# Queries and keys turned on VectorE and through DRAM, two groups ahead, from the 57th group on

## The chip, the cores and the metric

The kernel runs on one core of one Trainium2 chip. The metric is device time of one execution in microseconds. Everything is fp32. Engine names are those of the profile: PE is TensorE's matmul (PEld its weight loads), DVE VectorE, ACT ScalarE, POOL GpSimd; SP is the SyncE queue, from which all DMAs here are issued.

## The reference

Input x is [2, 4096, 256]. First comes a recurrent mixing layer (queries, keys and values from x and x shifted by one token, a running log-sum-exp over the 4096 tokens, a group norm, an output projection), added to x. Its result is normalised and goes through two layers of windowed attention with a gated MLP, and the sum is the output. Per layer (8 heads of 64, windows of 128 tokens, each window seeing itself and the one before):

```python
h = shift_token(x)
q, k, v = jnp.split(h @ wqkv, 3, axis=-1)        # 256 -> 3 x 512
q = l2norm(q) * qs;  k = l2norm(k) * ksc
q, k = rotary_xpos(q, k)
o = local_attention(q, k, v)                     # softmax over up to 129 keys
x = x + o @ wo
h = layernorm(shift_token(x)) ;  a, g = split(h @ w1 + b1)
x = x + (a * gelu(g)) @ w2 + b2
```

## The kernel before

**Work.** After the recurrence of the first batch (some 240 us, the kernel's start), the attention layers go over 128 groups of 128 tokens (NN = 128; group n is window n % 4 of block n // 4, four groups to a block of 512 tokens). The blocks run batch by batch, and in a batch layer by layer: 8 blocks of layer 0, then 8 of layer 1. The recurrence of the second batch is woven into groups 5 to 54.

**One group**, in the loop at L1540, written as iteration n: group n's scores, softmax and turning of probabilities; group n + 1's projection; group n - 1's fetch of turned probabilities; group n - 2's values, output projection and residual; and a part of the MLP of an earlier block (fill, L1412).

- project (L1033): 128 tokens times wqkv, 512 columns each for q, k and v, out of PSUM into qk (two buffers) or vt.
- square, rotate, norms, cosines, rotated (L1062 to L1104): norm and rotary position. ACT squares qk into the tile sq (one buffer); POOL multiplies the rotated halves into t2; DVE reduces sq to rn, POOL takes rn to the power -1/2; DVE writes the cosine products over sq, adds t2 to it, and writes sq times rn back into qk.
- transpose_qk (L1106): PE transposes qk in eight 128x128 blocks (four for k, four for q) into two PSUM banks, and ACT or DVE copies them into kT and qT. kT has three parts: 1 and 2 for even and odd groups; after an odd group part 2 is copied to part 0 by a DMA, so that a group always finds the window before it just ahead of its own.
- scores (L1130): 32 matmuls (64 records of fp32, as two passes) of 32 queries by 160 keys, eight at a time in parts of the array, and behind them, in one piece, values of group n - 2 (L1250).
- softmax (L1156), turn_p (L1203): the probabilities are transposed in 32x32 blocks on DVE (tile turned), written to DRAM (pd), and fetched in the turned order (fetch_p, L1226, four DMAs into pT; plan.turned, L250, is the view that does it). values reads pT and pB as its moving operand.
- shift, normed, transpose_h (L1287 to L1328): the shifted residual for the MLP, by four DMAs a group.

**Order.** No engine's order is written out by hand. Every call is noted as an operation of a plan (L274) with a cost (L338); order() (L412) runs all engines in a list schedule by those costs, picks at each step the operation of the lowest iteration among those that can start, gives out the eight PSUM banks and decides for "either" copies between ACT and DVE. The instructions are then written in that order, and each engine works through its own strictly in turn. A changed cost or a changed operation can so move instructions anywhere. A DMA's cost is this line, with 170 bytes a nanosecond:

```python
o.passes = size / 170 if ways == 16 else size / (25 * ways)
```

Nearly all instructions bear the line of the helper that writes them (L566), so groups are known by their tiles.

Of the kernel before, what the change touches and what calls it, by code (L numbers as in the profile page):

```python
# [33 lines left out]
MASKED = -3e38  # L34
R_SLOTS = 50
AHEAD = 10
SPLIT = 3
INSIDE = 2

# [154 lines left out]
class Plan:  # L194
# [143 lines left out]
    def cost(self, o):  # L338

        views = [*o.outs, *o.ins]  # L340
        n = max([v.idx.size for v in views] or [1])
        psum = any(v.place.psum for v in views)
        inside = sum(v.idx.size == n and not v.place.psum for v in o.ins)
        o.set, o.lock, o.half, o.passes, name, hold = None, False, "full", 0, o.name, None
        if o.eng == "tensor":
            trans = name == "transpose"
            left = o.args[1]
            move = o.args[2] if len(o.args) > 2 else o.args[1]
            cols = max(move.idx.size, left.idx.size) if not trans else P
            o.step = (1 if trans else 2) * (cols / 1.2 + (2 if cols >= 256 else 3))  # L350
            rows, cols = (P // max(n, 32) if n <= 64 else 1 for n in (left.shape[0], left.idx.size))
            if not trans and rows * cols > 1:
                o.half = "part" if rows > 1 and cols > 1 else "row" if rows > 1 else "col"
                o.step /= rows * cols
            o.time = o.step + 150
        elif o.eng == "vector":
            d = 150 + 1.04 * n
            if name == "tensor_tensor_reduce":
                d = 240 + 1.04 * n
            elif name == "tensor_tensor_scan":  # L360
                d, o.lock = 203 + 2.1 * n, True
            elif name == "scalar_tensor_tensor":
                d, o.lock = 200 + 1.05 * n, inside > 1
            elif name == "tensor_tensor":
                o.lock = inside > 1
            elif name == "tensor_scalar":
                d, o.lock = 155 + (1.27 if psum else 0.98) * n, not psum and n > 16
            elif name == "tensor_copy" and not psum:
                d, o.lock = 230 + 0.45 * n, n > 16
            elif name == "bn_aggr":  # L370
                d = 172
            elif name == "transpose":
                d = 170 + 1.04 * n
            elif name == "reciprocal":
                d = 147 + 4 * n
            o.step, o.time = max(d - 85, 60), d
        elif o.eng in ("scalar", "either"):
            d = (160 if psum else 195) + 0.83 * n
            if name == "scaled":
                d = 305 + 0.76 * n  # L380
            elif name == "activation":
                o.set = SETS.get(o.args[2])
                if o.args[2] == AF.Identity:
                    d = 365 + 0.87 * n
                elif isinstance(o.kw.get("bias"), View):
                    d += 85
            o.step, o.time = d - 100, d
            if "accum_out" in o.kw:
                o.time = d + 200
        elif o.eng == "gpsimd":  # L390
            o.lock = name != "memset"
            if name == "tensor_tensor":
                d = 430 + 156 * n if ALU.pow in o.args else 140 + 2.22 * n
            elif name == "tensor_scalar":
                d = 230 + 1.12 * n
            else:
                d = (100 if name == "memset" else 187) + 0.98 * n
            o.step, o.time = d, d
            hold = d if n > 64 else 100
        else:  # L400
            v = min(views, key=lambda v: v.shape[0] * v.idx.size)
            size = 4 * v.shape[0] * v.idx.size
            rows = max(v.shape[0] if v.shape[0] > 1 else v.shape[1] for v in views)
            ways = max(k for k in range(1, 17) if rows % k == 0)
            o.passes = size / 170 if ways == 16 else size / (25 * ways)
            inner = len(views) == 2 and not any(v.place.outer for v in views)
            o.step = 370 if not inner else 580 if ways in (1, 16) else 800
            o.time = LAND + o.passes
        o.hold = hold or o.time
# [160 lines left out]
def kernel(ctx: ExitStack, tc: tile.TileContext, a: dict, out: bass.AP):  # L570
# [331 lines left out]
    w2 = tile_of([P, NM, D], "w2")  # L902

    def weights(l, which):
        if "qkv" in which:
            for j in range(3):
                cols = slice(j * INNER, (j + 1) * INNER)
                nc.sync.dma_start(out=wqkv[:, :, cols], in_=a["w_qkv"][l][:, :, cols])
        if "o" in which:
            nc.sync.dma_start(out=wo, in_=a["w_o"][l])  # L910
        if "1" in which:
            nc.sync.dma_start(out=w1, in_=a["w_1"][l])
        if "2" in which:
            nc.sync.dma_start(out=w2, in_=a["w_2"][l])


    kT = tile_of([P, HEADS // 2, 3, W], "kT")

# [6 lines left out]
    G_LAST = 5  # L927
    blocks = [(l, b, c) for b in range(B) for l in range(L) for c in range(NB)]
    xs, xTs, hs, x1s, zs, hTs, rems, pys = ({} for _ in range(8))
    tabs, qks_of, vts, qTs, pos, sims, prs, pTs, pBs, dvs, sqs, t2s = ({} for _ in range(12))  # L930


    def load(k):
# [161 lines left out]
    def rotated(n):  # L1095
        qk = qks_of[n]
        (u, rn), t2 = sqs.pop(n), t2s.pop(n)
        nc.vector.tensor_tensor(u, u, t2, ALU.add)
        nc.vector.tensor_tensor(
            qk.rearrange("p j h d -> p (j h) d"),  # L1100
            u.rearrange("p j h d -> p (j h) d"),
            rn.unsqueeze(2).to_broadcast([P, 2 * HEADS, DH]),
            ALU.mult,
        )  # L1104

    def transpose_qk(n):  # L1106
        qk = qks_of.pop(n)
        qT = qTs[n] = tile_of([P, HEADS // 2, P], "qT", 2)
        me = 1 + n % 2
        for j, dst in ((1, kT[:, :, me, :]), (0, qT)):  # L1110
            pt = bank([P, HEADS // 2, P])
            for hp in range(HEADS // 2):
                nc.tensor.transpose(
# [1 line left out]
                    qk[:, j, 2 * hp : 2 * hp + 2, :].rearrange("p h d -> p (h d)"),  # L1115
                    ident,
                )
            either(dst, pt)
        if me == 2:
            nc.sync.dma_start(out=kT[:, :, 0, :], in_=kT[:, :, 2, :])  # L1120

    def lone(n):

# [6 lines left out]
    def scores(n):  # L1130

        qT = qTs[n]
        me = 1 + n % 2
        seen = W if lone(n) else 2 * W
        ks = slice(me, me + 1) if lone(n) else slice(me - 1, me + 1)
        sims[n] = [bank([P, 2, 2 * W]) for _ in range(4)]
        with piece():
            down_ends(n - 1)  # L1140
            for hp in range(HEADS // 2):
                for q, r in product(range(NQ), range(2)):
                    s, m = divmod(hp, 2)
                    rows, toks = slice(r * DH, (r + 1) * DH), slice(q * SQ, (q + 1) * SQ)
                    keys = slice(0, W) if lone(n) else slice(q * SQ, q * SQ + W + SQ)
                    nc.tensor.matmul(
                        sims[n][2 * s + r][toks, m, 2 * W - seen : 2 * W][:, keys],
                        qT[rows, hp, toks],
                        kT[rows, hp, ks, :].rearrange("p c j -> p (c j)")[:, keys],
                        start=True,  # L1150
                        stop=True,
                    )
# [375 lines left out]
    mixed_out(0)  # L1528
    transpose_x(0)
    load(1)  # L1530
    table(0)
    for j in range(3):
        project(0, j)
    square(0)
    rotate(0, 0)
    rotate(0, 1)
    norms(0)
    cosines(0)
    rotated(0)
    for n in range(NN + 3):  # L1540
        k, w = divmod(n, NW)
        o = n - 1
        ko, wo_ = divmod(o, NW)
        here, ahead, behind = n < NN, n + 1 < NN, 1 < n <= NN + 1
        plan.at(n)
        if here:
            transpose_qk(n)
        for c in range(rec2.n):
            if NW + 1 + int(c * R_SLOTS / rec2.n) == n:
# [7 lines left out]
                    rec2.group_norm()  # L1557
        plan.at(n)

        first, l = ahead and (n + 1) % (NB * NW) == 0, ((n + 1) // (NB * NW)) % L  # L1560
        if w == 3 and k + 2 < NK:
            load(k + 2)
        if w == 0 and k + 1 < NK:
            mixed_out(k + 1)
        if n > 2:
            normed(hs[(n - 3) // NW][:, (n - 3) % NW, :])
        if ahead:
            table(n + 1)
            if first:
                weights(l, "qkv")  # L1570
            project(n + 1, 0)
            rotate(n + 1, 0)
        if here:
            scores(n)
        else:
            with piece():
                if n < NN + 2:
# [7 lines left out]
        if here:  # L1585
            softmax(n, 0)
            softmax(n, 1)
        if ahead:
            project(n + 1, 1)
            square(n + 1)  # L1590
            rotate(n + 1, 1)
        if behind:
            output(n - 2)
            shift(n - 2)
# [1 line left out]
                weights(o // (NB * NW) % L, "o")  # L1596
        if wo_ == 1 and 0 < ko < NK:
            transpose_h(ko - 1)
        if w == 2 and k + 1 < NK:
            transpose_x(k + 1)  # L1600
        if here:
            softmax(n, 2)
            softmax(n, 3)
        if ahead:
            norms(n + 1)
        fill(o, 0)
        if here:
            turn_p(n, 0)
        if ahead:
            project(n + 1, 2)  # L1610
            cosines(n + 1)
        fill(o, 1)
        if here:
            turn_p(n, 1)
        if ahead:
            rotated(n + 1)
        fill(o, 2)
        fill(o, 3)
        if wo_ < 2 and NW < o < NN and (o - NW - wo_) % (NB * NW) == 0:
# [83 lines left out]
```

## Time and profile before

| | us |
|---|---|
| median of 3 runs | 2783.24 (2782.43 to 2784.07) |
| profiled execution, its own time | 2785.52 |
| its span | 2783.8 |
| PE / DVE / ACT / POOL busy in it | 2741.1 / 2173.9 / 1894.2 / 1676.8 |
| scores of group 0 / 56 / 127 begin | 243.1 / 1364.5 / 2708.1 |

A group's length is the distance between the starts of two bursts of kT,qT matmuls on PE's timeline. It varies from 13 to 23 us with the share of the MLP that falls into it. The granted TensorE clock is 0.995 over the span. In rows of groups the columns are: line, engine, operation, out<-in, shapes, count, then busy us and mean ns of one, then the idle time of the engine just before them and what ended it. Matmuls are pipelined: the length of one record overlaps the next.

### The profile page before, as it was taken

To read this page: it belongs to the slowest core of one execution; us is meant where nothing else is said; L and a number is where in the kernel's file an instruction comes from. 1 tells how busy PE (TensorE), PEld (TensorE's weight loads), DVE (VectorE), ACT (ScalarE), POOL (GpSimd) and SP (SyncE) were. 2 spreads that over 40 slices of the span, in tenths; PEclk is the share of its full clock that TensorE was granted. 3 is DMA by queue.
4 is the path that set the end of the run, shared out by engine and by line. 5 is a ranking of instruction groups with operands and counts; after the bars stand their busy time and mean duration, and the time that the engine had idled before them with its cause. 6 is when DMAs were issued, how large, how long until landed. Compare 5 with 4: busy or idle time off the path is not lost.

```text
span 2783.8 us, 61393 instructions
## 1 busy us (share of the span) xinstructions
PE 2741.1 (98%) x21356; PEld 1752.8 (63%) x21356; DVE 2173.9 (78%) x4651; ACT 1894.2 (68%) x5079; POOL 1676.8 (60%) x1959
## 2 busy tenths in 40 slices
PE   9999999999999999999999999999999999999998
PEld 4476656656666666666666666666665666666666
DVE  7888989998988888888776776677776777776663
ACT  7887767777777776676666666666666666666663
POOL 2226666667666666766665665666666666666661
PEclk9999999999999999999999999999999999999999
DMA  2224535444443444333435443343334444334331
GB/s 82 104 69 166 174 108 156 124 121 135 138 127 101 144 115 121 106 99 114 121 117 153 131 151 115 110 122 110 114 104 125 138 130 118 113 117 123 108 100 47
DMA packets 414365, 332.13 MB, mean 119 GB/s; under 512 B 61412, under 2 KB 377572, under 8 KB 413544
## 3 DMA queue, kind: packets, MB, share of 16 engines
q1 hardware_dynamic: 414056, 328.20, 39.5%
q8 instruction: 170, 2.79, 0.4%
q14 instruction: 139, 1.14, 0.1%
HBM read 153.01 MB, written 108.99 MB: 94 GB/s over the span
## 4 chain that ended last, share of the span: by engine, by line
PE 80%; DVE 2%; ACT 2%; issue 0%; DMA 0%; POOL 0%; SPq 0%; DVEq 0%; ACTq 0%
PE bank L566 80%; ACT pr L566 1%; DVE arena L566 1%; DVE qk L566 0%; ACT pr L562 0%; ACT arena L566 0%; DVE sq L566 0%; ACT L566 0%; DVE turned L566 0%; DVE hm L566 0%; ACT hm L566 0%; DVE rn L566 0%; ACT oT L566 0%; DVE bank L566 0%; ACT ends L566 0%
## 5 line engine op out<-in xcount | busy, mean ns | idle before, releaser
L566 PE MATMUL bank<-wqkv,xT 128*128 128x512 f32 x1536 | 711.8, 597 | 4.5 <-POOL xT L566 4.0
L566 PE MATMUL bank<-hT,w 128*128 128x512 f32 (+2 forms) x1452 | 636.3, 582 | 0.0
L566 POOL TENSOR_TENSOR t<-qk,tab 128x256 f32<-128x256 f32 x512 | 393.4, 788 | 278.5 <-ACT qk L566 228.8
L566 PEld LDWEIGHTS bank<-wqkv,xT 128*128 128x128 f32 x1536 | 280.4, 191 | 284.9 <-issue 269.4
L566 ACT ACTIVATE pr<-bank,nmx 128x129 f32<-128x129 f32 (+1 forms) x1024 | 367.7, 379 | 130.3 <-DVE nmx L566 113.5
L566 PEld LDWEIGHTS bank<-hT,w 128*128 128x128 f32 (+1 forms) x1452 | 269.7, 189 | 274.0 <-issue 254.0
L566 POOL TENSOR_TENSOR rn<-rn,mhalf 128x16 f32<-128x16 f32 x128 | 390.8, 3053 | 5.7
L562 ACT ACTIVATE pr<-pr,sums 128x129 f32<-128x129 f32 (+1 forms) x972 | 325.3, 421 | 19.5 <-DVE sums L566 19.2
L566 POOL TENSOR_SCALAR_AFFINE_SELECT pB<-pT 127x512 f32<-127x512 f32 x248 | 238.3, 976 | 143.0 <-DMA pT<-pd 105.7
L566 DVE COPY_PREDICATED bank<-fronts,bank 128x254 f32<-128x254 int32 x496 | 187.8, 418 | 171.6 <-PE bank L566 171.2
L566 ACT COPY qk<-bank 128x512 f32<-128x512 f32 x222 | 130.5, 588 | 250.2 <-PE bank L566 232.6
L566 PE MATMUL bank<-w,hm 128*128 128x256 f32 x1280 | 298.5, 382 | 0.0
L566 PEld LDWEIGHTS bank<-w,hm 128*128 128x128 f32 x1280 | 237.8, 190 | 35.6 <-issue 6.0
L566 PE MATMUL bank<-wo,oT 128*128 128x256 f32 x1024 | 242.5, 380 | 1.4 <-ACT oT L566 1.3
L566 PEld LDWEIGHTS bank<-wo,oT 128*128 128x128 f32 x1024 | 194.1, 190 | 58.1 <-issue 19.6
L566 DVE STREAM_TRANSPOSE turned<-pr 128x512 f32<-128x512 f32 (+1 forms) x380 | 195.2, 538 | 40.4 <-ACT pr L562 38.7
L566 ACT ACTIVATION_READ_ACCUMULATOR pr<-bank,nmx 128x1 f32 x1024 | 221.5, 216 | 0.0
L566 ACT COPY hm<-bank 128x512 f32<-128x512 f32 (+1 forms) x175 | 100.8, 576 | 175.0 <-PE bank L566 174.9
L566 DVE TENSOR_REDUCE rn<-sq 128x16 f32<-128x1024 f32 x128 | 155.0, 1211 | 71.1 <-ACT sq L566 69.9
L566 PE MATMUL bank<-pT,vt 128*64 128x128 f32 x2048 | 203.4, 279 | 0.0
L566 POOL TENSOR_TENSOR dv<-dv,vt 127x512 f32<-127x512 f32 x124 | 177.0, 1428 | 30.4 <-DMA dv<-vt 23.4
L566 DVE TENSOR_REDUCE nmx<-bank 128x2 f32<-128x258 f32 x496 | 192.6, 413 | 0.1
(154 smaller groups left out, 5106.2 us busy)
## 6 DMA issues: line engine op xcount, KB each, us to landing
pd<-turned SPq DMA_DIRECT2D x256, 256.0 KB
pT<-pd SPq DMA_DIRECT2D x512, 128.0 KB
dv<-vt SPq DMA_DIRECT2D x124, 224.0 KB
tab<-in_c_rot_dram SPq DMA_DIRECT2D x128, 128.0 KB
kT<-kT SPq DMA_DIRECT2D x64, 256.0 KB
z<-zd SPq DMA_DIRECT2D x16, 512.0 KB
x<-in_x_dram SPq DMA_DIRECT2D x16, 512.0 KB
x1d<-x SPq DMA_DIRECT2D x16, 512.0 KB
```

Source lines behind the costliest of these rows:

```text
L562: self.nc.scalar.activation(dst, src, AF.Copy, scale=scale)
L566: getattr(getattr(self.nc, o.eng), name)(*args, **kw)
```

## The change

Up to group 55 all stays as it was, but for the layout of kT and qT: both are now cut into blocks of 32 tokens (block, head pair, token) where they were (head pair, part, token), and the copies out of PSUM write that layout.

From group 56 on (FAR = 56):

- Iteration n projects q and k of group n + 2 instead of n + 1 (v stays at n + 1), with all steps up to rotated. At iteration 54 the chain of group 56 is done once more, whole (rotated_now), to start this off.
- transpose_qk is gone. In its place turn_qk, right behind rotated: two transposes on DVE in 32x32 blocks, qk (q, then k) into the tile sq, whose content is no longer wanted, and one DMA of the 512 KB to a DRAM buffer qd (three of them).
- fetch_qk, right behind the scores of the iteration before its own: eight DMAs of 64 KB out of qd, four into kT and four into qT, each for one block of 32 rows, in runs of 512 bytes.
- A block's x is transposed one group sooner (w == 1 in place of 2). At a change of layer the weights of q and k are loaded apart from those of v, since they are wanted a group apart.

For all groups, the plan's cost of a DMA goes from 170 to 270 bytes a nanosecond. The sum of DVE transposes added is 144, of DMAs 72 writes and 576 fetches, of PE transposes removed 576.

```diff
+FAR = 56
-            o.passes = size / 170 if ways == 16 else size / (25 * ways)
+            o.passes = size / 270 if ways == 16 else size / (25 * ways)
...
-    kT = tile_of([P, HEADS // 2, 3, W], "kT")
+    kT = tile_of([P, 3 * NQ, HEADS // 2, SQ], "kT")
+    qds = [plan.dram([P, 2 * INNER], f"qd_{i}") for i in range(3)]
...
     def rotated(n):
+        turns[n] = u
...
+    def rotated_now(n):
+        table(n)
+        project(n, 0)
+        project(n, 1)
+        square(n)
+        rotate(n, 0)
+        rotate(n, 1)
+        norms(n)
+        cosines(n)
+        rotated(n)
...
+    def turn_qk(n):
+        qk, u = qks_of.pop(n), turns.pop(n).rearrange("p j h d -> p (j h d)")
+        for j in range(2):
+            to = u.rearrange("p (b j c) -> p b j c", b=NQ, j=2)[:, :, j, :]
+            of = qk[:, j].rearrange("p h d -> p (h d)")
+            nc.vector.transpose(
+                to.rearrange("p b (h t) -> p b h t", t=SQ),
+                of.rearrange("p (h b d) -> p b h d", b=NQ, d=SQ),
+            )
+        nc.sync.dma_start(out=qds[n % 3], in_=u)
+
+    def fetch_qk(n):
+        qT = qTs[n] = tile_of([P, NQ, HEADS // 2, SQ], "qT", 2)
+        for b in range(NQ):
+            bs = slice(b * SQ, (b + 1) * SQ)
+            for j, dst in ((1, kT[bs, mine(n)]), (0, qT[bs])):
+                nc.sync.dma_start(
+                    out=dst.rearrange("p a h t -> p a (h t)"),
+                    in_=plan.turned(qds[n % 3], (2 * b + j) * P, 0, P),
+                )
+        kept_keys(n)
...
+    def kept_keys(n):
+        if n % 2:
+            nc.sync.dma_start(out=kT[:, :NQ], in_=kT[:, 2 * NQ :])
...
                     nc.tensor.matmul(
-                        sims[n][2 * s + r][toks, m, 2 * W - seen : 2 * W][:, keys],
-                        qT[rows, hp, toks],
-                        kT[rows, hp, ks, :].rearrange("p c j -> p (c j)")[:, keys],
+                        sims[n][2 * s + r][toks, m, o : o + wide * SQ],
+                        qT[rows, q, hp, :],
+                        kT[rows, b0 : b0 + wide, hp, :],
...
+        m = n + 1 if n + 1 < FAR else n + 2
+        comes = m < NN
         plan.at(n)
-        if here:
+        if n < min(FAR, NN):
             transpose_qk(n)
...
-        if ahead:
-            table(n + 1)
-            if first:
-                weights(l, "qkv")
-            project(n + 1, 0)
-            rotate(n + 1, 0)
+        if comes:
+            table(m)
+            if m % (NB * NW) == 0:
+                weights(m // (NB * NW) % L, "qk")
+            project(m, 0)
+            rotate(m, 0)
         if here:
             scores(n)
+            if FAR <= n + 1 < NN:
+                fetch_qk(n + 1)
...
-        if w == 2 and k + 1 < NK:
+        if w == (1 if (k + 1) * NW >= FAR else 2) and k + 1 < NK:
             transpose_x(k + 1)
...
-        if ahead:
-            rotated(n + 1)
+        if comes:
+            rotated(m)
+            if m >= FAR:
+                turn_qk(m)
+        if n + 2 == FAR:
+            rotated_now(FAR)
+            turn_qk(FAR)
```

More of the change, by code (lines that the diff above doesn't have):

```diff
@@ L904, in weights @@
     def weights(l, which):
-        if "qkv" in which:
-            for j in range(3):
+        for j, t in enumerate("qkv"):
+            if t in which:
                 cols = slice(j * INNER, (j + 1) * INNER)
@@ L929 @@
     xs, xTs, hs, x1s, zs, hTs, rems, pys = ({} for _ in range(8))
-    tabs, qks_of, vts, qTs, pos, sims, prs, pTs, pBs, dvs, sqs, t2s = ({} for _ in range(12))
+    tabs, qks_of, vts, qTs, pos, sims, prs, pTs, pBs, dvs, sqs, t2s, turns = ({} for _ in range(13))
     def load(k):
@@ L1104, in rotated @@
         )
+    def rotated_now(n):
[8 more added lines that the diff above has]
+        rotated(n)
     def transpose_qk(n):
         qk = qks_of.pop(n)
-        qT = qTs[n] = tile_of([P, HEADS // 2, P], "qT", 2)
-        me = 1 + n % 2
-        for j, dst in ((1, kT[:, :, me, :]), (0, qT)):
+        qT = qTs[n] = tile_of([P, NQ, HEADS // 2, SQ], "qT", 2)
+        for j, dst in ((1, kT[:, mine(n)]), (0, qT)):
             pt = bank([P, HEADS // 2, P])
@@ L1117, in transpose_qk, with mine @@
                 )
-            either(dst, pt)
-        if me == 2:
-            nc.sync.dma_start(out=kT[:, :, 0, :], in_=kT[:, :, 2, :])
+            either(dst.rearrange("p a h t -> p h a t"), pt.rearrange("p h (a t) -> p h a t", t=SQ))
+        kept_keys(n)
[10 more added lines that the diff above has]
+    def fetch_qk(n):
+        qT = qTs[n] = tile_of([P, NQ, HEADS // 2, SQ], "qT", 2)
+        for b in range(NQ):
[5 more added lines that the diff above has]
+                )
+        kept_keys(n)
+    def mine(n):
+        me = 1 + n % 2
+        return slice(me * NQ, (me + 1) * NQ)
+    def kept_keys(n):
+        if n % 2:
+            nc.sync.dma_start(out=kT[:, :NQ], in_=kT[:, 2 * NQ :])
     def lone(n):
@@ L1130, in scores @@
     def scores(n):
[L1134 to L1137, printed above, removed]
+        qT = qTs.pop(n)
         sims[n] = [bank([P, 2, 2 * W]) for _ in range(4)]
@@ L1144, in scores @@
                     rows, toks = slice(r * DH, (r + 1) * DH), slice(q * SQ, (q + 1) * SQ)
-                    keys = slice(0, W) if lone(n) else slice(q * SQ, q * SQ + W + SQ)
+                    own = mine(n).start
+                    b0, wide = (own, NQ) if lone(n) else (own - NQ + q, NQ + 1)
+                    o = W if lone(n) else q * SQ
                     nc.tensor.matmul(
-                        sims[n][2 * s + r][toks, m, 2 * W - seen : 2 * W][:, keys],
-                        qT[rows, hp, toks],
-                        kT[rows, hp, ks, :].rearrange("p c j -> p (c j)")[:, keys],
+                        sims[n][2 * s + r][toks, m, o : o + wide * SQ],
+                        qT[rows, q, hp, :],
+                        kT[rows, b0 : b0 + wide, hp, :],
                         start=True,
@@ L1530 @@
     load(1)
[L1531 to L1539, printed above, removed]
+    rotated_now(0)
+    project(0, 2)
     for n in range(NN + 3):
@@ L1558 @@
         plan.at(n)
-        first, l = ahead and (n + 1) % (NB * NW) == 0, ((n + 1) // (NB * NW)) % L
         if w == 3 and k + 2 < NK:
@@ L1587 @@
             softmax(n, 1)
-        if ahead:
-            project(n + 1, 1)
-            square(n + 1)
-            rotate(n + 1, 1)
+        if comes:
+            project(m, 1)
+            square(m)
+            rotate(m, 1)
         if behind:
@@ L1603 @@
             softmax(n, 3)
-        if ahead:
-            norms(n + 1)
+        if comes:
+            norms(m)
         fill(o, 0)
@@ L1609 @@
         if ahead:
+            if (n + 1) % (NB * NW) == 0:
+                weights((n + 1) // (NB * NW) % L, "v")
             project(n + 1, 2)
-            cosines(n + 1)
+        if comes:
+            cosines(m)
         fill(o, 1)
@@ L1614 @@
             turn_p(n, 1)
-        if ahead:
-            rotated(n + 1)
+        if comes:
+            rotated(m)
[4 more added lines that the diff above has]
+            turn_qk(FAR)
         fill(o, 2)
```

## The prediction

> **What bounds the kernel now.** I read the views in this order: the page's engine table and chain of waits, the windows by stage, the groups by form, PE's timeline over two groups of the steady part, and the DMA issues of the SP queue. The page first:
>
> ```profile
> span 2783.8 us, 61393 instructions
> PE 2741.1 (98%) x21356; PEld 1752.8 (63%) x21356; DVE 2173.9 (78%) x4651; ACT 1894.2 (68%) x5079; POOL 1676.8 (60%) x1959
> PE 80%; DVE 2%; ACT 2%; issue 0%; DMA 0%; POOL 0%; SPq 0%; DVEq 0%; ACTq 0%
> ```
>
> PE is busy almost throughout and carries the chain that ended last; the next owners of that chain have 2% each. An average may hide stages, so the windows come next. Group 56, the first that the change treats otherwise, begins its scores at 1364.5 us (the 57th burst of kT,qT matmuls on PE's timeline), group 124 at 2657.5. Columns: length, busy us of each engine, granted clock, share of the DMA engines, GB/s.
>
> ```profile
> 400.00:1364.50 964.50, 954.17 (x7684) 611.08 (x7680) 847.55 (x1738) 709.54 (x1900) 628.68 (x715) 0.99 0.42 122
> 1364.50:2658.00 1293.50, 1293.50 (x10805) 826.94 (x10807) 928.87 (x2062) 828.69 (x2381) 829.13 (x927) 1.00 0.41 122
> 2658.00:2783.80 125.80, 117.22 (x900) 82.59 (x884) 59.45 (x137) 56.74 (x168) 41.60 (x48) 0.97 0.26 77
> ```
>
> In the middle row PE is busy 1293.50 of 1293.50 us: for 68 groups it never waits, whatever the others do. A group lasts 1293.5 / 68 = 19.02 us there; DVE works 928.87 / 68 = 13.66 us of it (72%), ACT and POOL 12.2 us each (64%). So in this stage time is PE's work, and only what leaves PE's list counts, as long as the other engines keep it fed.
>
> **What the change takes from PE.** Eight 128x128 transposes a group (transpose_qk) for groups 56 to 127: 72 x 8 = 576, and the instruction lists of the two programs differ on PE by just these. Their price must not be read from the mean of one (274 ns, the first row below), which counts a pipelined instruction from start to end, nor from busy time / count (131 ns), which has the last one's tail in it. It is the distance between starts on PE's timeline (start, length, what, count):
>
> ```profile
> L566 PE MATMUL bank<-mats,qk 128*128 128x128 f32 x1024 | 134.2, 274 | 9.7 <-DVE qk L566 9.7
> ...
> 1805.07 1.34 PE L566 MATMUL bank<-kT,qT 64*32 64x160 f32 x64
> 1806.34 0.44 PE L566 MATMUL bank<-pT,vt 128*64 128x128 f32 x4
> 1806.61 0.39 PE L566 MATMUL bank<-pB,dv 128*64 128x128 f32 x4
> 1806.83 0.39 PE L566 MATMUL bank<-pT,vt 128*64 128x128 f32 x4
> 1807.05 0.39 PE L566 MATMUL bank<-pB,dv 128*64 128x128 f32 x4
> ...
> 1825.54 1.04 PE L566 MATMUL bank<-mats,qk 128*128 128x128 f32 x8
> 1826.41 1.88 PE L566 MATMUL bank<-wqkv,xT 128*128 128x512 f32 x4
> ```
>
> From 1825.54 to 1826.41 the eight take 0.87 us of PE; the same 0.87 stands at nearly every group after 1000 us. 72 x 0.87 = **62.6 us** less PE work.
>
> The Trainium skill speaks against such a change: "VectorE: DVE Perf Modes", Rules for kernel authors, gives 128x128 transposes to TensorE where a PSUM destination will do, and The three transpose paths there puts one at 390 ns in bf16. By that figure 576 of them would be an estimated 225 us of PE; this trace's starts, 109 ns apart, decide for 62.6.
>
> **The scores with the new layout (all 128 groups).** Keys are now read as four or five pieces of 32 floats, 512 bytes apart, in place of one run. The nearest row is pT/pB: they are read as four pieces of 32, 1 KB apart, and four records of 128 columns, two side by side, start 0.22 us apart: 4 x 128 / 2 / 0.22 = 1160 columns per us, where 512 contiguous columns take 0.43 us (1190). So pieces cost nothing that shows. Value taken: 0. Bounds: 0, and half speed, 1.25 us a group (64 records, median distance of starts) x 128 = 160 us.
>
> **What goes to the others, from group 56 on.** Prices by these rows:
>
> ```profile
> L566 DVE STREAM_TRANSPOSE turned<-pr 128x512 f32<-128x512 f32 x256 | 180.8, 706 | 40.4 <-ACT pr L562 38.7
> L566 ACT COPY kT<-bank 128x512 f32<-128x512 f32 x115 | 67.5, 587 | 29.9 <-PE bank L566 29.2
> ...
> 1832.97 1.52 SPq L566 DMA_DIRECT2D pT<-pd  x3
> 1838.23 0.53 SPq L566 DMA_DIRECT2D pd<-turned  x1
> ```
>
> - DVE gains two block transposes of 128x512 (turn_qk): 2 x 0.706 = 1.41 us, so 13.66 + 1.41 = 15.07 us. The group shrinks to 19.02 - 0.87 = 18.15 us: 83%.
> - ACT loses nearly all of two copies out of PSUM, 2 x 0.59 = 1.18 us, and two PSUM banks are free earlier. ACT falls to 11.0 of 18.15 us (61%). No gain is counted: ACT is not the bound.
> - SP issues nine more DMAs: one write of 512 KB (as pd<-turned, 0.50 us each over this stage) and eight fetches (as pT<-pd, 0.48): 4.4 us. Added up over 1364 to 2700 us its issues hold 753 us of SP, 10.7 us a group; they become 15.1 of 18.15, again 83%.
> - The DMA engines: 1024 packets of 512 B (27.6 ns each, mean of such packet records here) and 128 of 4 KB (189 ns) are 52 us, over 16 engines 3.3 us a group. The share goes from 0.41 to (0.41 x 19.02 + 3.3) / 18.15 = 0.61.
> - POOL keeps its work.
>
> **New idle time of PE.** None of this is on PE, and the projection two groups ahead gives the turned keys a whole group to arrive. But all engines run in a written order and DVE is fuller. The trace has both ends: at 72% DVE PE idles 0; between 400 and 1364.5 us, with DVE at 847.55 / 964.5 = 88%, it idles 10.33 us in 48 groups, 0.21 a group. At 83% a straight line gives 0.15 a group, 72 x 0.15 = **10.7 us**. Bounds: 0, and 1 us in each of some 36 short groups, half of the 72 (rival 1). If the cover is gone, each microsecond of wait per group costs 72.
>
> **The other edits.** The planner's DMA rate (170 to 270) and the new copies reorder the whole program, the first 1364 us too; the 10.3 us of PE idle there may halve or double: -5 to +10, taken as 0, since a reordering has no sign that I can read. At iteration 54 a whole extra chain for group 56 (rotated_now) falls where DVE is at 88%: its DVE work, some 6.8 us (1.21 + 2 x 0.73 + 1.34 + 1.34 + 1.41), comes sooner, not on top; 0 to 5 us, taken as 0 because PE has a group's work ahead of it. The weights loaded in two parts: before, PE idles nothing at groups 64 and 96; 0. The fewer DMA pieces of the kept keys: off the path, 0. In the last 125.8 us PE idles 8.6; projecting earlier leaves PE less to fill with there, up to +3, in the range.
>
> **Sum.** The profiled execution took 2785.52 us, 1.7 more than its span; the median shown is 2783.24. All terms are differences of span, so they are put on the median: 2783.2 - 62.6 + 10.7 = **2731.3 us**.
>
> **Rivals.**
> 1. *SP becomes the late one.* For: 15.1 us of issues against short groups (from the scores of 56 to those of 57 it was 13.7 us, and one or two in four are 13 to 17), while pT, dv and the eight fetches all become ready together just behind the scores, 8.5 us in one queue. Against: the long groups, 20 to 23 us, let it catch up, and SP idles 45% now. If each of the 36 short groups loses 1 us: 2731 + 36 = 2767.
> 2. *The one sq buffer closes a loop (slower than before).* The turned block lies in sq, and the next group's square on ACT has to wait until the write to DRAM has read it. Behind square in ACT's order stand the exponentials, and behind those the scores' banks and PE. The loop: square 1.07, reduction 1.21, POOL's power 0.44 + 3.05, product 1.34, turning 1.41, issue 0.50, landing some 3.6 (pT<-pd 2.56 in the chain, plus 1.5 - 0.4 for the larger transfer, an estimate from the packet records): 12.6 us. It binds when waits in DVE's, ACT's and SP's queues add over 18.15 - 12.6 = 5.5 us a group, and from 6.4 us on the result is slower than before. With 7 us of waits a group takes 19.6: 2783 + 72 x 0.58 = 2825. Against: two of three queues have 17% free, the third 39%.
> 3. *Keys in pieces run slower*: half speed would be 2731 + 160 = 2891. The pT row speaks against it.
> 4. *The change doesn't do what it says*: PE finds other waits at once, and the time stays at 2783. Against: 68 groups without a gap.
>
> **The numbers.** My forecast case (2715 to 2748) has 0.72; below it, with the early idle gone too, 0.03; rival 1 and the upper part of its cost (2748 to 2777) 0.10; rival 4 (within 0.2%, about what a measurement can tell from no change: 2777.7 to 2788.8) 0.04; rival 2 has 0.09, rival 3 0.02. Faster 0.72 + 0.03 + 0.10 = 0.85, same 0.04, slower 0.11. The low end is 2783.2 - 62.6 - 5 = 2715; the upper end goes to rival 1's 2767, so that about 2 in 10 stay outside.
>
> **What would show it.** Right: 448 transposes (mats,qk) left on PE in place of 1024, PE still over 98% busy between group 56 and 124 with some 18.2 to 18.4 us a group, sq<-qk transposes near 0.7 us, kT,qT still 1.25 us a group, the DMA share near 0.6. Wrong: PE idle before kT,qT released by DMA kT<-qd (rival 1), ACT idle before sq released by DMA qd<-sq (rival 2), or kT,qT over 1.4 us a group (rival 3). The prediction fails most easily at the 0.15 us of idle a group, which is a line drawn through two points.

## The result, and the profile after

The changed kernel took 2813.99 us (median of 4, 2807.84 to 2818.15), the kernel before 2783.64 (4 runs, 2782.43 to 2784.07): ratio 1.0108, 95% interval 1.0087 to 1.0129. It is **slower by 30 us**; 2731.3 with a range up to 2767 was forecast. Below, each measured time is followed by its ratio and the 95% interval of it; differences in us are differences of such ratios, each to the kernel before on the same chip, times 2783. By the intervals such a difference is uncertain by some 6 us.

The page of the changed kernel:

```profile
span 2806.1 us, 60848 instructions
PE 2708.9 (97%) x20780; PEld 1703.0 (61%) x20780; DVE 2274.6 (81%) x4814; ACT 1818.0 (65%) x4916; POOL 1683.2 (60%) x1959
PE 6%; DVE 3%; SPq 3%; ACT 3%; DMA 2%; issue 1%; POOL 1%; POOLq 0%; DVEq 0%; ACTq 0%
```

PE has 576 instructions less, as forecast. But the chain that ended last, followed back over some 19% of the span here, is no longer PE's (80% of the span before): SP, DVE and ACT have half of PE's share each, and DMAs 2%. By stage (length, busy us of PE, PEld, DVE, ACT, POOL, granted clock, DMA share, GB/s):

```profile
397.00:1349.50 952.50, 947.14 (x7765) 609.21 (x7764) 845.95 (x1742) 703.68 (x1890) 625.79 (x711) 1.00 0.42 125
1349.48:2676.14 1326.66, 1268.36 (x10226) 780.83 (x10225) 1027.71 (x2205) 761.72 (x2237) 842.57 (x929) 0.99 0.58 172
```

The first row ends sooner than before (group 56 starts its scores at 1349.5 instead of 1364.5). The second, groups 56 to 123, was 1293.0 us (1364.5 to 2657.5) with PE busy throughout; now it is 1326.7 and PE idles 58.3 us. So the stage that should have shrunk by 59 grew by 34. The two largest waits of PE there (us in total, times, longest):

```profile
PE bank L567 <- ACT oT L567: 24.3, 14, 3.4
PE bank L567 <- DMA qT<-qd: 18.9, 16, 2.5
```

The second row is the fetch itself arriving late. The first is something else: output projections that wait for ACT's copy of oT. Why ACT is late is seen further up the stream. DVE's longest list of waits in this stage, after:

```profile
DVE st L567 <- DMA h<-x: 133.5, 48, 7.5
```

and in the same groups before:

```profile
DVE st L566 <- DMA h<-x: 63.5, 14, 5.8
```

h<-x is the shifted residual of the MLP, four pieces a group, a transfer that the change does not touch. One such case, on all engines' timeline of the changed kernel (start, length, engine, what, count, [idle before <- releaser]):

```profile
2071.22 1.20 SPq L567 DMA_DIRECT2D h<-x  x2
2072.51 1.08 SPq L567 DMA_DIRECT2D pd<-turned  x2
2073.68 0.40 SPq L567 DMA_DIRECT2D kT<-qd  x1
...
2076.99 0.43 SPq L567 DMA_DIRECT2D qT<-qd  x1
...
2077.47 1.46 SPq L567 DMA_DIRECT2D h<-x  x2
...
2080.32 0.43 DVE L567 BATCH_NORM_STATS2 st<-h 128x6 f32<-128x256 f32 x1 [3.03 <-DMA h<-x]
...
2082.10 1.31 DVE L567 STREAM_TRANSPOSE sq<-qk 128x512 f32<-128x512 f32 x2
...
2083.33 0.72 DVE L567 COPY_PREDICATED bank<-fronts,bank 128x254 f32<-128x254 int32 x2
...
2084.47 0.37 ACT L567 ACTIVATE pr<-bank,nmx 128x129 f32<-128x129 f32 x1 [5.58 <-DVE nmx L567]
...
2084.83 0.58 ACT L567 COPY oT<-bank 128x512 f32<-128x512 f32 x1
...
2085.46 1.35 PE L567 MATMUL bank<-wo,oT 128*128 128x256 f32 x5 [0.74 <-ACT oT L567]
```

Read it down. Two pieces of h are issued at 2071.2; then the eight fetches hold SP from 2073.68 to 2077.42, back to back, and the last two pieces of h come only behind them. DVE's statistics of h wait 3.03 us for those. DVE works in turn, so what stands behind the statistics is late: the two added transposes, then the mask of the scores and the maximum (nmx); ACT's exponentials, 5.58 us idle, wait for nmx; behind them in ACT's order stands the copy of oT; and there PE runs dry. No single wait is long on PE, but it is the end of a chain of four in-order engines that begins in SP's queue.

This is not one case alone. In 40 of the 48 waits, DVE goes on at most 1.2 us after SP has finished the last issue of h<-x before; in the kernel before, 9 of its 14 waits end so. Most often, then, h is late because it is issued late, not because it takes longer to land. And each wait of PE can be followed back, from releaser to releaser, to the first DMA on its way: of the 57.6 us in waits longer than 0.15 us, 24.9 lead to h<-x, 20.8 to the fetches themselves, 7.3 to z<-zd (a transfer of 512 KB that the change does not touch) and 2.5 to dv<-vt.

The issues of SP in this stage, added up by rows of its timeline (short gaps within a row included), hold it for 1000 of 1326.7 us (75%, 14.7 us a group, 1842 issues); before, 720 of 1293 (56%, 1230 issues). The granted clock of the span is 0.992, the half clock coming in spells of 3.4 or 6.8 us after PE's waits: 0.008 x 2806 = 22 us of full-clock work, 15 of them in this stage.

### The profile page after: what moved, and what is told of

Read it like the earlier page. It is cut to its first block, busy times and chain, and to the rows that moved or that the text cites. A ratio compares the mean times of both kernels' runs of the same rounds, so it can differ in the third digit from the quotient of the medians.

```text
span 2806.1 us, 60848 instructions
## 1 busy us (share of the span) xinstructions
PE 2708.9 (97%) x20780; PEld 1703.0 (61%) x20780; DVE 2274.6 (81%) x4814; ACT 1818.0 (65%) x4916; POOL 1683.2 (60%) x1959
## 5 line engine op out<-in xcount | busy, mean ns | idle before, releaser
L567 POOL TENSOR_TENSOR t<-qk,tab 128x256 f32<-128x256 f32 x512 | 422.4, 843 | 154.5 <-ACT qk L567 115.3
L567 POOL TENSOR_SCALAR_AFFINE_SELECT pB<-pT 127x512 f32<-127x512 f32 x248 | 200.4, 823 | 256.5 <-DMA pT<-pd 133.7
L567 PE MATMUL bank<-kT,qT 64*32 64x160 f32 (+1 forms) x8192 | 184.6, 303 | 25.9 <-DMA qT<-qd 21.6
L567 PE MATMUL bank<-pB,dv 128*64 128x128 f32 x1984 | 196.9, 278 | 5.4 <-POOL dv L567 5.4
L567 DVE TENSOR_TENSOR sq<-qk,tab 128x512 f32<-128x512 f32 x256 | 198.4, 801 | 1.1
```

The costliest lines, as they stand in the source:

```text
L567: getattr(getattr(self.nc, o.eng), name)(*args, **kw)
```

## The experiments

There are four theories. **S** (Q, or Qi, in the expectations): SP's queue; too many issues in one row hold up other transfers. **D**: DVE is too full (the step of my forecast). **L**: the loop through the one sq buffer (rival 2). **B** (Qb in the expectations): the bytes, which take the DMA engines from others or arrive late themselves. Theory P, in some expectations, is that the planner's order is wrong. The reordered early part counts apart from these.

### What the whole trip costs, and what the rest gives

*Without the trip*: the write to qd and the eight fetches are left out (kT and qT keep old contents from group 56 on); projection ahead and DVE's turning stay.

```diff
-        nc.sync.dma_start(out=qds[n % 3], in_=u)
...
-                nc.sync.dma_start(
-                    out=dst.rearrange("p a h t -> p a (h t)"),
-                    in_=plan.turned(qds[n % 3], (2 * b + j) * P, 0, P),
-                )
```

> Leaves out the write of the turned block to DRAM and its eight fetches (the scores then use whatever stands in kT and qT); all else of the change stays, the two DVE transposes too. Theory Q (the one SP queue is too full: nine more issues a group, 4.1 us, make h, qT and kT land late): 2784 - 62.6 + some 5 = about 2727 us, PE dense again. Theory D (DVE, 1.34 us fuller, is the late engine): about 2810, as the change itself, since DVE's work is the same. Theory L (the single sq buffer, held until its write to DRAM has read it): about 2727 too, since the write is gone.

Measured: 2708.11, ratio 0.9727 (0.9713 to 0.9742).

```profile
1345.65:2580.83 1235.18, 1234.41 (x10225) 769.18 (x10224) 1034.67 (x2242) 750.89 (x2202) 853.91 (x928) 1.00 0.43 127
```

PE is dense again, 1234.41 of 1235.18 us, 18.16 us a group, with DVE at 1034.67 / 1235.18 = 84%. DVE's wait for h<-x falls from 133.5 us to 12.0, and the clock is 0.999:

```profile
DVE st L567 <- DMA h<-x: 12.0, 12, 2.5
```

Theory D forecast 2810 here, with DVE's work unchanged; that work is unchanged (1034.67 us against 1027.71), and the loss is gone. The trip costs 1.0108 - 0.9727 = 3.81%, **106 us**, 1.47 a group.

*The layout and the planner's rate alone* (no group is treated the new way):

```diff
-FAR = 56
+FAR = 1000
```

> FAR set beyond the last group, so that only the new layout of kT and qT and the planner's DMA rate of 270 are left; PE transposes all 128 groups. By the prediction's terms for these (0 and 0): 2783 us. If the layout or the new order had a part in the loss: above 2790. The run without the trip came out 75 us below before where 62.6 were priced, so the new order may be worth some 10 us: then 2773.

Measured: 2767.08, 0.9949 (0.9934 to 0.9963), 14 us better than before; group 56 begins at 1348.1. From here to the kernel without the trip is 62 us: the removed transposes, forecast 62.6, and all else that comes with them. In groups 56 to 123 alone, where PE is dense in both runs, it is 1292.1 - 1235.2 = 56.9 us, forecast 68 x 0.87 = 59.2. The three steps go from kernel to kernel, so that they add up, -14 - 62 + 106 = +30, is no check; that the middle one meets the forecast is.

*The rate alone*, in the kernel before:

```diff
-            o.passes = size / 170 if ways == 16 else size / (25 * ways)
+            o.passes = size / 270 if ways == 16 else size / (25 * ways)
```

> The kernel before with the planner's DMA rate of 270 bytes per ns alone. The run with the new layout and this rate, and PE's transposes kept, came out 15 us below before. If the rate (a new order) is what gained: about 2767. If the layout did (fewer pieces in the copy of the kept keys, other copies): 2783.

Measured: 2777.91, 0.9982 (0.9972 to 0.9991): 5 us of the 14.

### Not DVE, not the loop

*DVE relieved*: the two transposes cut to 32 columns each (keys and queries are then mostly not turned), 0.9 us less of DVE a group.

```diff
+            nc.vector.transpose(u[:, j * SQ : (j + 1) * SQ], of[:, :SQ])
```

> The two DVE transposes of 128x512 a group are cut to 128x32 (0.19 us each in place of 0.67), so the scores get untransposed rows; DMAs, buffers and dependences stay. DVE is relieved by 1.0 us a group. Theory D: most of the loss goes, 2814 - 72 x 1.0 = about 2745 us. Theory Q: SP keeps its 29 issues a group, so about 2805, with DVE still waiting for DMA h<-x by over 100 us. Theory L: 2805 or so, the buffer is held nearly as long.

Measured: 2822.49, 1.0143 (1.0126 to 1.0160). No gain, and the waits for h<-x are longer, 177.5 us. It is not a clean test: in the new order SP stands at the head of its queue until the write to qd has landed, 69.6 us in this stage, where the changed kernel has 0.2:

```profile
SPq L567 <- DMA qd<-sq: 69.6, 37, 4.3
```

Theory D falls by the run without the trip.

*A second sq* for odd groups, in free room of the arena:

```diff
+        if n > FAR and n % 2:
+            sq = sqs[n] = plan.view(arena, 0, [P, 2, HEADS, DH])
```

> A second sq buffer for every other group from 57 on, in the arena that the recurrence has left, so that the next square need not wait for the write to DRAM. Theory L (rival 2 of the prediction): the waits go and the time falls to about 2740 us. Theories Q and D: ACT waited for DMA qd<-sq only 12 us in the whole stage, so no more than those: 2800 to 2814.

Measured: 2822.46, 1.0139 (1.0123 to 1.0156). No gain. Here too SP stands 68.9 us waiting for the writes (43.5 for qd<-sq, 25.4 for qd<-arena), so by itself this run does not decide. In the changed kernel, ACT's square waits for qd<-sq 12.2 us in all, and the write alone (below) keeps the one buffer and its wait for the write, 9.0 us, with PE dense: by that run theory L falls.

### The queue

*The kernel before with nine more issues a group*, 2 KB each, from group 56 on; its PE transposes stay and nothing waits for the added DMAs:

```diff
+        if n >= 56:
+            for i in range(9):
+                nc.sync.dma_start(out=more[9 * (n % 3) + i], in_=qTs[n][:32, 0, :16])
```

> The kernel before, with its transposes on PE, and nine more DMAs a group from group 56 on, of 2 KB each (32 rows of 64 bytes out of qT into DRAM places that nobody reads), right behind the scores. Nothing waits for them but SP's queue and the next write of qT. Theory Qi: SP goes from 10.6 to some 14.5 us a group and its late landings stop PE: slower than before, 2783 + about 40 us. Theory Qb: 2 KB are nothing, so 2783 to 2788.

Measured: 2835.59, 1.0195 (1.0178 to 1.0212), 54 us slower, with almost no bytes (DMA share 0.42, before 0.41).

```profile
1360.81:2703.69 1342.88, 1308.17 (x10774) 832.19 (x10773) 914.53 (x2055) 833.55 (x2387) 818.02 (x927) 0.99 0.42 118
```

```profile
DVE st L566 <- DMA h<-x: 164.2, 42, 11.5
```

The changed kernel's illness appears in the old one: SP's issues hold it 78%, DVE waits 164.2 us for h in place of 63.5, and PE, dense before, idles 34.7, of which 28.6 lead back to h<-x. The added DMAs also wait for qT at the head of the queue (SP's waits for ACT's qT: 157.6 us, before 96.6), so the 54 us are issue time and waiting at the head together.

*Four fetches in place of eight*: queries and keys lie side by side, so that one DMA of 128 KB brings both.

```diff
+    kq = plan.view(arena, 2 * INNER, [P, 3 * NQ, 2, HEADS // 2, SQ])
...
+            nc.sync.dma_start(
+                out=kq[b * SQ : (b + 1) * SQ, mine(n)].rearrange("p a j h t -> p a (j h t)"),
+                in_=plan.turned(qds[n % 3], 2 * b * P, 0, 2 * P),
+            )
```

> Four fetches of 128 KB in place of eight of 64 KB: queries and keys of a group lie side by side in one tile (in the arena, from group 56 on), and one DMA brings the 32 rows of both. Same bytes, packets of 1 KB in place of 512 B, SP relieved by 4 x 0.45 = 1.8 us a group. Theory Q: 40 per cent of the added issue time goes, and since waits in a queue grow faster than its load, half or more of the 92 us lost: about 2765 us. Theories D and L: 2805 to 2814.

Measured: 2769.00, 0.9954 (0.9940 to 0.9969).

```profile
1350.89:2638.57 1287.68, 1247.50 (x10213) 773.37 (x10212) 1022.07 (x2200) 757.75 (x2230) 837.58 (x925) 0.99 0.60 177
```

The same bytes (DMA share 0.60) with four issues less: **43 us** better. The packets are 1 KB in place of 512 B, but what they take of the DMA engines has not fallen (0.60 x 1287.7 = 773 us, before 0.58 x 1326.7 = 769). SP is held 69% and DVE waits for h 99.1 us.

*The eight fetches from ACT's queue*:

```diff
+            far = name == "dma_start" and any(v.place in self.far for v in o.ins)
+            getattr(getattr(self.nc, "scalar" if far else o.eng), name)(*args, **kw)
```

> The eight fetches a group are issued from ACT's queue instead of SP's, at the same places of the order; bytes and packets unchanged. SP loses 3.6 us a group, ACT (11.2 of 19.5 us busy) gains them. Theory Qi: SP is back at 11.4 us a group, ACT at 14.8 of 18.2; about 2740 us if ACT's in-order stream bears it. Theory Qb: no gain, 2800 or more.

Measured: 2766.45, 0.9940 (0.9926 to 0.9955), 47 us better than the change and no better than merging. SP falls to 60%, but ACT pays. Its waits (whole span):

```profile
ACT hm L568 <- DMA qT<-qd: 14.9, 6, 4.7
ACT hm L568 <- DMA kT<-qd: 13.4, 6, 3.9
```

The activation hm uses neither tile: what waited was a fetch ahead of it in ACT's order, for an earlier DMA. All such waits hold ACT for some 70 us.

*Merged and from ACT's queue*:

> The merged fetch (four of 128 KB) and its issue from ACT's queue together. SP is then back near the run without the trip (58 per cent busy), and ACT carries four issues a group in place of eight. Theory Qi: below both single steps (2769 and 2766), some 2730 us; what is left over the 2708 of no trip is ACT's four issues of 0.5 us in an in-order stream. If the two gains are the same one, it stays at 2760 to 2770.

Measured: 2767.59, 0.9950 (0.9938 to 0.9963). I had expected the two to add; they don't. The stage takes 1283.34 us against 1287.68. DVE's waits for h fall to 71.0 us, less than with the layout alone (83.4, PE idle 1.3), and yet PE idles 39.7: the sum of the waits for h is no measure of the loss.

### The bytes

*Few bytes, nine issues*: write and fetches keep their count, with 8 of every 128 columns (32-byte packets; the rest of kT and qT stays old).

```diff
+        few = lambda t: t.rearrange("p (x c) -> p x c", c=P)[:, :, :8]
+        nc.sync.dma_start(out=few(qds[n % 3]), in_=few(u))
```

> The change with the same nine DMA issues a group and the same order of steps, but each carries a sixteenth of its bytes (32 bytes of every 512), so most of kT and qT stays stale. Theory Qi (what costs is that SP issues them one after another, some 0.45 us each): about 2805 us, as the change. Theory Qb (what costs is their bytes, which make all landings later): about 2715, near the run without the trip (2708).

Measured: 2839.45, 1.0206 (1.0191 to 1.0221): no gain with 1/16 of the bytes, SP at 76%. It is not a clean test of the bytes: SP now waits 85.4 us at the head of its queue for the write to land (0.2 us in the changed kernel), so it only shows that few bytes do not help while the queue is this full.

*Merged and few bytes*: the four fetches and the write with 32 columns (at most 1/8; keys and queries mostly old).

```diff
+        nc.sync.dma_start(out=qds[n % 3][:, :SQ], in_=u[:, :SQ])
```

> The merged fetches (2769) with the same five issues a group and an eighth of the bytes or less: the write carries 128 bytes of each row's 4 KB, each fetch 128 bytes of every 1 KB, so most of the queries and keys are stale. If the bytes are what is left of the loss: 2725 or below. If the five issues in SP's order and what waits for them are: 2755 to 2775.

Measured: 2723.80, 0.9783 (0.9766 to 0.9799).

```profile
1348.93:2601.06 1252.13, 1239.72 (x10225) 770.72 (x10225) 1033.55 (x2230) 752.09 (x2213) 831.94 (x925) 1.00 0.47 130
```

48 us better than merged with all bytes: once the queue is relieved, the bytes do count. One way shows in the traces: with all bytes only 14 of DVE's 44 waits for h end within 1.2 us of the last issue of h (median 1.5 us), with few bytes 17 of 29 (median 1.1). What is left to the kernel without the trip is 16 us.

*The write alone* (the fetches are left out, so keys and queries are old):

> The turned block is written to DRAM (one issue, 512 KB a group) but never fetched; the scores use what stands in kT and qT. By issues: one of nine, 2708 + 106 / 9 = about 2720. If the large write in itself delays the transfers behind it (h, pd, pT): 2735 or more.

Measured: 2709.74, 0.9733 (0.9719 to 0.9748): the 512 KB written cost 2 us, within the uncertainty nothing, and less than either theory had.

```profile
1347.52:2582.78 1235.26, 1233.91 (x10226) 769.40 (x10225) 1031.97 (x2198) 761.02 (x2247) 856.42 (x928) 1.00 0.51 156
```

DMA share 0.51 and PE dense. So it is not bytes as such but, as far as these runs go, the fetches' bytes. They start right behind the scores, where pT, dv and h are due too, and the next scores wait for them; that this is why they cost and the write does not is argued, not shown.

*Merged, fetched half an iteration later*:

```diff
+                plan.at(n + 0.5)
                 fetch_qk(n + 1)
+                plan.at(n)
```

> Merged fetches on SP (2769), with the fetches ranked half an iteration later in the plan, so that SP puts h, pT and pd of the same iteration first where both can start. If the place of the fetches in SP's queue is what hurts h: 2750 or less. If the number of issues and bytes is, wherever they stand: 2765 or more, with PE waiting for arena<-qd instead.

Measured: 2793.26, 1.0036 (1.0022 to 1.0051), 23 us worse than merged. h is relieved (DVE waits 47.4 us for it), but now the scores themselves come up against the fetch:

```profile
PE bank L567 <- DMA arena<-qd: 35.4, 35, 3.1
```

This one attempt to move the fetch out of the burst made it late.

### The planner's idea of an issue

The planner counts 370 ns for an issue to or from DRAM; in the changed kernel's stage a fetch out of qd holds SP for 450 ns in the mean. With 480:

```diff
-            o.step = 370 if not inner else 580 if ways in (1, 16) else 800
+            o.step = 480 if not inner else 580 if ways in (1, 16) else 800
```

in the changed kernel,

> The change as it is, but the planner is told that a DMA issue to or from DRAM holds SP for 480 ns in place of 370 (the traces show 0.45 to 0.53 us), so that it lays out the order for the SP that there is. Theory P (the loss is a wrong order: the plan believed in an SP that is 25 per cent faster): 2750 us or less. Theory Qi (29 issues in turn, in whatever order, hold up the transfers between): 2800 or more.

2796.51, 1.0052 (1.0035 to 1.0068); in the merged one,

> Merged fetches on SP (2769 alone) and the planner's issue cost at 480 ns. If the order is what is left (the plan believes in a faster SP than there is): as the same with the fetches on ACT (2752) or below. If SP's load in itself is what is left: 2765 or more, 17 us at most better than without.

2756.03, 0.9906 (0.9891 to 0.9920); merged and from ACT's queue,

> Merged fetches, issued from ACT, and the planner's issue cost at 480 ns. Theory P: better than the same without the cost (some 2730) by 10 us or more. Theory Qi: the same within 10 us, since SP is no longer full.

**2751.77, 0.9883 (0.9867 to 0.9900)**; merged and from POOL's queue,

> Merged fetches issued from POOL's queue, issue cost 480 ns in the plan. If what keeps the ACT version at 2752 is that waits for fetches stand in ACT's stream before the exponentials (some 45 to 70 us of waits there): POOL, 64 per cent busy and not ahead of PE, bears them better, about 2730. If POOL's own issue of a DMA takes it a microsecond or more, POOL (12.4 + 4 of 18.2 us) becomes late with rn and pB: 2780 or more.

2765.43, 0.9939 (0.9924 to 0.9954); and with the layout alone (no trip, PE's transposes),

> No trip at all: the layout, the rate of 270 and PE's transposes (2767 without more), with the issue cost at 480 ns. If the truer cost is worth something by itself, below 2760; if it only matters where SP is full, 2767 within 3 us. It says how much of the 17 us belongs to SP's load.

2782.03, 1.0000 (0.9990 to 1.0009). With a trip, 480 gains 16, 13 and 19 us; without one it loses 14. By stage, in the profiled executions (us, at 370 and at 480):

| | scores of group 56 begin | groups 56 to 123 |
|---|---|---|
| the change | 1349.5, 1357.0 | 1326.7, 1307.9 |
| merged | 1350.9, 1357.3 | 1287.7, 1267.2 |
| merged, from ACT | 1352.6, 1359.9 | 1283.3, 1266.0 |
| layout alone, no trip | 1348.1, 1358.7 | 1292.1, 1296.7 |

All four lose 6 to 11 us before group 56. In the stage with the trip the three gain 17 to 21, and without the trip 5 are lost. So a mere reordering is worth some 15 us in this kernel, and no difference of that size above (the losses with the smaller transposes and with the second sq, the remaining 16) should be given a cause. That in this stage the truer cost gains only where the trip's issues are suits theory S but doesn't prove it. The kernel merged and from ACT's queue, planned with 480, is the best that computes everything: 33 us faster than before and 63 faster than the change. It does not reach the layout's 14 plus the transposes' 62.

## Why the prediction was wrong

- **New idle time of PE** is the step that failed. I had 10.7 us, from a line through two points of DVE's share. The no-trip run has DVE at 84% and PE idle 0.8 us in 68 groups: DVE's share was the wrong variable. With the trip the idle is 58.3 us, and another 34 us are on PE's busy time (1268.4 against 1234.4). Spells of half clock behind the waits make 15 of these 34, a cost that the line left out though the stretch it was drawn from had lost 5 us to it (clock 0.99 in its row); where the other 19 come from is not shown. My sentence "None of this is on PE" was true, and not enough: the nine issues were in the queue that h goes through, and h reaches PE by way of DVE and ACT.
- **Rival 1** was the mechanism, at the wrong price. I had the SP figures right (15.1 us a group forecast, 14.7 measured) and the burst of 8.5 us behind the scores, but asked only when the fetches would be late, not what stood behind them. The sign that I named, PE waiting for a fetch, is there with 18.9 + 1.9 us; a somewhat larger part, 24.9 us, leads back to h<-x through the engines between. Its price was 36 us, 1 us in every other group; the trip measures 106, of which halving the fetches' number takes 43 and cutting their bytes and the write's 48 more.
- **SP idles 45% now** was my evidence against it. A share over long and short groups says nothing about a queue that is filled in bursts.
- **The transposes**: 62.6 us forecast, 62 between two runs, 56.9 of 59.2 in groups 56 to 123. The distance of starts was the right row. The estimate of 225 us from the Trainium skill's 390 ns ("VectorE: DVE Perf Modes", The three transpose paths) was not: one after another the transposes start 109 ns apart here, fp32 as they are.
- **The turning on DVE**: 0.706 us forecast; the profile's tile view of sq (least/median/most ns) has

```profile
L567 DVE STREAM_TRANSPOSE sq<-qk x136: 657/671/712, 1356.1 to 2660.7; 128x512 f32<-128x512 f32 x136
```

- **Keys in pieces** (rival 3): 19.9 ns from record to record in bursts without a wait, 19.5 before: nothing, as taken.
- **The DMA share**: 0.61 forecast, 0.58 measured.
- **The loop** (rival 2): no; the write alone keeps it and costs nothing that shows.
- **The other edits**, taken as 0 within -5 to +10: the layout and the rate gave -14. Outside the range, to the good. In the profiled executions group 56 begins 16 us sooner; PE idles 7 us less up to there (26.9 against 34.1) and half clock takes 8 less (1.7 against 10.2). I had counted only the idle time from 400 us on, and no clock.

Open: how much of the 48 us of the fetches' bytes is h landing later, when as many written bytes cost 2; and why moving the merged fetches to ACT's queue gained only 1 us at the one issue cost and 6 at the other, no more than the uncertainty, though ACT is busy for some 60% of the stage and its issues hold it for another 8%.

## What to carry to other kernels

Price an added DMA also as an instruction in the queue that issues it: look at what is issued behind it in the same burst, and follow that from engine to engine until something meets the bound. Few and large DMAs are worth more there than free bandwidth suggests. And here an engine that was 84% busy left the bound dense while a queue held 75% did not: my reading is that it matters whether the work comes evenly or in a row, ahead of something that is wanted now.

## What the runs showed of the hardware

- One issue held SP, in the mean of the changed kernel's stage, for 0.45 us (kT<-qd, qT<-qd), 0.67 (h<-x) and 0.72 (dv<-vt). On ACT's queue merged fetches took 0.3 to 0.4, on POOL's 0.56 (medians).
- Short waits of PE can cost more than their length, because half clock can follow them. In the changed kernel's stage the granted clock falls to half in eight spells (seven of 3.4 us, one of 6.8). Each begins 2.2 to 4.4 us after the start of a wait of PE, or of two close together, of 1.8 us or more in all; four other waits of 1.8 to 2.6 us were followed by none. Two cases, the first in the changed kernel, the second in the kernel before: eight wo,oT matmuls, elsewhere 1.89 us, stand with 3.65 behind an idle of 3.42 us, and eight hT,w matmuls, elsewhere 3.60, with 5.25 behind 5.33:

```profile
2491.87 3.65 PE L567 MATMUL bank<-wo,oT 128*128 128x256 f32 x8 [3.42 <-ACT oT L567]
```

```profile
1810.06 1.89 PE L566 MATMUL bank<-wo,oT 128*128 128x256 f32 x8
1811.79 3.60 PE L566 MATMUL bank<-hT,w 128*128 128x512 f32 x8
...
2720.28 1.62 PE L566 MATMUL bank<-w,ends 64*32 64x256 f32 x16 [5.33 <-DVE ends L566]
2721.82 5.25 PE L566 MATMUL bank<-hT,w 128*128 128x512 f32 x8
```

The granted clock is half from 2491.8 to 2495.2 us in the first case and from 2718.1 to 2724.9 in the second. The spans' granted clocks are 0.999 without the trip (2.7 us of clock lost, 0.001 x 2706) and 0.992 with it (22 us): some 20 of the trip's 106 us are this.
